# Grouped attention: the norm by half block, two scalings instead of four, turned outputs copied by ScalarE

## The chip, the cores and the metric

The kernel runs on one core of one Trainium2 chip. The metric is device time in microseconds (us) of one execution; a kernel's time is the median of several executions. The engines are TensorE (PE, with its weight loads PEld), VectorE (DVE), ScalarE (ACT), GpSimd (POOL) and SyncE (SP), which issues most DMAs.

## The reference

The program computes a decoder of two layers on x of 64 sequences x 64 steps x 256 channels, float32. Each layer adds three blocks to x, each on a layer norm of x:

```python
x = x + _L0_attn_ref(_layernorm(x), ...)    # Mamba-2 scan
x = x + _L0_xattn_ref(_layernorm(x), ctx_512, ...)   # latent cross attention
x = x + _L0_ffn_ref(_layernorm(x), ...)     # mixture of 7 experts, 2 chosen, 1 shared
x = x + _L1_attn_ref(_layernorm(x), ...)    # RWKV scan (WKV)
x = x + _L1_xattn_ref(_layernorm(x), ctx_512, ctx_512)
x = x + _L1_ffn_ref(_layernorm(x), ...)     # grouped mixture, 8 of 64 chosen
```

The change is in the fifth of these, the grouped attention of layer 1, which has no weights: 32 query heads of 8 channels share 8 key and value heads, taken from the 64 channels of ctx_512:

```python
qh = q.reshape(B, S, KV, G, D).transpose(0, 2, 3, 1, 4)     # KV 8, G 4, D 8
kh = k.reshape(B, S, KV, D).transpose(0, 2, 1, 3)
vh = v.reshape(B, S, KV, D).transpose(0, 2, 1, 3)
weights = jax.nn.softmax(jnp.einsum('bkgsd,bktd->bkgst', qh, kh) / scale, axis=-1)
out = jnp.einsum('bkgst,bktd->bkgsd', weights, vh)
```

## The kernel before

The residual x stays in SBUF for the whole program: 4096 tokens as 32 tiles of 128 tokens on the partitions. Four tiles are a block (8 blocks of 512 tokens), two tiles a half (16 halves of 256). A tile is two sequences of 64 steps.

The work of a layer is written as many Python generators, called streams. `Plan.play` (L204) runs them against each other while the program is built: each stream says at its `yield` which marks, which PSUM banks or which rank it waits for, the planner keeps an estimated time at which each engine is free, and the ready stream that could begin first continues, ties by rank. The order in which instructions are issued on each engine is fixed in that way; on the chip an engine takes its own instructions in that order. So an edit to one stream can move the instructions of all others. All instructions are recorded through one helper, so the profile gives line 62 for each; they are told apart by the names of their tiles.

Layer 1 (`layer1`, L1664) plays together: the WKV streams (`wkv_front`, `wkv_scan`, names wk_ and wn_), one pair for each half; the grouped attention (`gqa_front`, one for each block, and `gqa_tile`, one for each tile); the mixture (`ffn_front`, names fn_ and fr_; `ffn_half`, `ffn_gate`, `ffn_down`, names gu_ps, aT, acc); and the collection of layer 0's expert outputs by gathers of GpSimd (x_sb<-moe_ys). The mark ("scan", h) is set when WKV's result of half h is added to x, ("keys", b) when the keys kb of block b are there, ("gqa", n) when attention of tile n is added, ("ffn", n) when the mixture's result of tile n is added. `after` leaves out marks with a negative number. GQA_LEAD is 9: attention of tile n waits for the mixture of tile n-9.

`gqa_tile` (L1336) does for tile n:

- it waits for the block's keys, the half's scan, the attention of tile n-2 and the mixture of tile n-9;
- it calls `norm` (L287) for one tile: statistics gn_st and gn_mv on VectorE, variance plus epsilon gn_rs on VectorE, its power -1/2 on GpSimd, and gn_nm, minus the mean times that, on VectorE;
- GpSimd clears two columns of each query group in one of three buffers gqa_q, and scales x into it by four `tensor_scalar`, one for each of the four query heads g that share a key head (128 partitions x 64 columns each);
- `gqa_turned` (L1324): four PE transposes pq, copied to qT by ScalarE;
- 32 small score matmuls sc into four banks, whose maxima VectorE writes, negated, into the cleared columns of gqa_q; a second `gqa_turned` (qT2), so that the second score matmuls st contain the maximum; ScalarE's exponentials pT;
- eight matmuls pv with the values and a column of ones; VectorE copies the result from PSUM to oT; four transposes po; VectorE divides (rc, at); GpSimd adds to x.

`norm` takes the first tile and the number of tiles, keeps st in one buffer and mv, rs, nm in two, and yields between its steps. Other blocks call it for two or four tiles at a time.

Of the kernel before, what the change touches and what calls it, by code (L numbers as in the profile page):

```python
# [8 lines left out]
ALU = mybir.AluOpType  # L9
# [6 lines left out]
NT = TB // P  # L16
# [5 lines left out]
GQA_LEAD = 9  # L22
# [18 lines left out]
def bc(ap, axis, n):  # L41

    ap = ap.unsqueeze(axis)
    shape = list(ap.shape)
    shape[axis] = n
    return ap.to_broadcast(shape)
# [193 lines left out]
class Net:  # L240
# [1083 lines left out]
    def gqa_turned(self, wk, qa, tag):  # L1324
# [8 lines left out]
        yield [4]  # L1333
        return qT

    def gqa_tile(self, wk, w, n, f):  # L1336
        nc, te, v, gp = self.nc, self.nc.tensor, self.nc.vector, self.nc.gpsimd
        t = n % NT
        yield self.after(("keys", n // NT), ("scan", n // 2), ("gqa", n - 2), ("ffn", n - GQA_LEAD))
        r_ = {}  # L1340
        yield from self.norm(wk, n, 1, "gn", r_)
        qa = w["q"][n % len(w["q"])]
        gp.memset(qa.rearrange("p g k c -> p (g k) c")[:, :, 16:18], 0.0)
        xg = self.x[:, n].rearrange("p (k j g d) -> p g k j d", k=4, j=2, g=4)
        for g in range(4):
            gp.tensor_scalar(qa[:, g, :, 0:16].rearrange("p k (j d) -> p k j d", j=2), xg[:, g], r_["rs"], r_["nm"], ALU.mult, ALU.add)
        qT = yield from self.gqa_turned(wk, qa, "qT")

        sc = [self.mm([P, 4, 2, S], "sc") for _ in range(4)]
        for g in range(4):  # L1350
            for k in range(4):
                r = slice(32 * k, 32 * k + 32)
                for j in range(2):
                    te.matmul(sc[k][j * S:(j + 1) * S, g], qT[r, g, j * S:(j + 1) * S], f["kb"][r, 2 * t + j], start=True, stop=True)
        yield
        for k in range(4):
            v.tensor_reduce(qa[:, :, k, 16:18], sc[k], AX.X, ALU.max, negate=True)
        self.give(*sc)
        qT = yield from self.gqa_turned(wk, qa, "qT2")
        ps = [self.mm([P, 2, 4, S], "st") for _ in range(4)]  # L1360
        for j in range(2):
            for k in range(4):
                r = slice(32 * k, 32 * k + 32)
                te.matmul(ps[k][:, j], f["kb"][r, 2 * t + j].rearrange("p j t -> p (j t)"), qT[r, :, j * S:(j + 1) * S], start=True, stop=True)
        yield
        pT = wk.tile([P, 4, 2, 4 * S], F32, tag="pT", bufs=2, name="pT")
        for k in range(4):
            nc.scalar.activation(pT[:, k], ps[k].rearrange("p j g s -> p j (g s)"), AF.Exp, scale=8.0 ** -0.5)
        self.give(*ps)
        yield [1]  # L1370

        pv = self.mm([P, 4, 2, S], "pv")
        for j in range(2):
            for k in range(4):
                te.matmul(pv[k * 32:(k + 1) * 32, :, j], f["vb"][:, 2 * t + j, k].rearrange("p q d -> p (q d)"), pT[:, k, j],
                          start=True, stop=True)
        yield
        oT = wk.tile([P, 4, P], F32, tag="oT", bufs=2, name="oT")
        v.tensor_copy(oT, pv.rearrange("p g j s -> p g (j s)"))
        self.give(pv)  # L1380
        yield [1]
        po = self.mm([P, 4, 8, 16], "po")
        for g in range(4):
            te.transpose(po[:, g].rearrange("p k d -> p (k d)"), oT[:, g], self.ident)
        yield
        rc = wk.tile([P, 4, 8], F32, tag="rc", bufs=2, name="rc")
        v.reciprocal(rc, po[:, :, :, 8])
        at = wk.tile([P, D], F32, tag="at", bufs=2, name="at")
        v.tensor_mul(at.rearrange("p (k g d) -> p g k d", k=8, g=4), po[:, :, :, 0:8], bc(rc, 3, 8))
        self.give(po)  # L1390
        yield
        gp.tensor_add(self.x[:, n], self.x[:, n], at)
        self.plan.mark("gqa", n)
# [270 lines left out]
    def layer1(self, wk, w_wkv, w_gqa, w_ffn):  # L1664
        self.wkv_padded(wk, w_wkv)
        streams = [(0, self.shared(n)) for n in self.shared_left] + [(1, x) for x in [self.load_ffn(w_ffn), self.prep_ffn(wk, w_ffn)]]
        fs = [{} for _ in range(NH + NBLK)]
        streams += [(n, self.collect(n)) for n in range(NH)]
        for n in range(NH):
            streams += [(n, self.wkv_front(wk, w_wkv, n, fs[n])), (n, self.wkv_scan(wk, w_wkv, n, fs[n]))]  # L1670
        for b in range(NBLK):
            g = fs[NH + b]
            streams.append((2 * b, self.gqa_front(wk, w_gqa, b, g)))
            streams += [(2 * b + t // 2, self.gqa_tile(wk, w_gqa, NT * b + t, g)) for t in range(NT)]
        for i, (n0, nt) in enumerate(self.GROUPS):
            f = {}
            streams.append((n0 // 2, self.ffn_front(wk, w_ffn, i, n0, nt, f)))
            streams += [(h, self.ffn_half(wk, w_ffn, i, h, f)) for h in range(n0 // 2, (n0 + nt) // 2)]
        with self.tc.manual_schedule():
            self.plan.play(streams)  # L1680
# [113 lines left out]
```

## Time and profile before

| | us |
|---|---|
| median of 3 timed runs | 2126.09 (2123.85 to 2131.75) |
| the profiled execution | 2121.44 |
| its span, first to last instruction | 2119.7 |
| first instruction of grouped attention (gn_st) | starts at 1161.7 |
| last addition of grouped attention to x | starts at 2008.2 |

| engine | busy us in the span | share |
|---|---|---|
| TensorE, matmuls | 1933.7 | 91% |
| VectorE | 1343.7 | 63% |
| ScalarE | 791.1 | 37% |
| GpSimd | 845.6 | 40% |

In a timeline line the first number is the start in us, the second the time taken, then engine, line, operation, what is written and read, and the count; in brackets the idle time of the engine before it and what ended that. In a list of waits the instruction left of the arrow waited for the one on its right. In a table of stages each engine has its busy time and, in brackets, its instructions; then come the clock granted to TensorE (1.00 is full), the busy share of the DMA engines, and GB/s.

### The profile page before, as it was taken

How to read it: one execution, taken by the hardware profiler on the slowest of the kernel's cores; microseconds unless marked ns; L12 is line 12 of the kernel's file. 1: busy time of each engine (PE TensorE's matmuls, PEld its weight loads, DVE VectorE, ACT ScalarE, POOL GpSimd, SP SyncE). 2: the span in 40 equal slices, each digit the busy share in tenths (PEclk: the TensorE clock that was granted, in tenths of full speed). 3: DMA queues.
4: the chain of work that ended last, by engine and by line, in shares of the span. 5: the costliest groups of instructions: out<-in, count | busy, mean ns of one | idle time of the engine just before them, and what ended most of it. 6: DMA issues, size and time to landing. Idle time of an engine off the chain costs nothing. (4 is left out here: it accounts for less than half of the span.)

```text
span 2119.7 us, 36371 instructions
## 1 busy us (share of the span) xinstructions
PE 1933.7 (91%) x13735; PEld 1548.6 (73%) x13735; DVE 1343.7 (63%) x3149; ACT 791.1 (37%) x1439; POOL 845.6 (40%) x1045
## 2 busy tenths in 40 slices
PE   7989898898989897899988879989899999999998
PEld 6768677687778775688876557767677777777777
DVE  5667776767676773343336887877778676755331
ACT  3425343434334332244433423433334334243220
POOL 2332434343534423111126856667456334432211
PEclk9989999999899998999998879989999999999999
DMA  7963200000000001388844212121111101010010
GB/s 206 348 202 118 67 16 22 16 22 16 22 26 26 22 31 67 132 302 281 276 159 91 29 21 35 15 35 22 22 20 24 19 14 18 9 23 15 17 23 11
DMA packets 167807, 150.43 MB, mean 71 GB/s; under 512 B 76153, under 2 KB 155408, under 8 KB 167632
## 3 DMA queue, kind: packets, MB, share of 16 engines
q1 hardware_dynamic: 152464, 121.61, 19.6%
q0 software_dynamic: 15168, 26.50, 5.1%
q8 instruction: 109, 1.79, 0.3%
q14 instruction: 66, 0.54, 0.1%
HBM read 88.01 MB, written 60.04 MB: 70 GB/s over the span
## 5 line engine op out<-in xcount | busy, mean ns | idle before, releaser
L62 PE MATMUL gu_ps<-hT,ffn_gu 128*128 128x256 f32 x1408 | 337.0, 386 | 5.0 <-DVE gqa_q L62 4.1
L62 PEld LDWEIGHTS gu_ps<-hT,ffn_gu 128*128 128x128 f32 x1408 | 260.2, 192 | 50.4 <-issue 8.4
L62 PE MATMUL acc<-ffn_d,aT 128*128 128x256 f32 x704 | 166.0, 389 | 9.2 <-DVE aT L62 9.2
L62 POOL TENSOR_TENSOR aT<-aT,ffn_sc 128x512 f32<-128x512 f32 (+1 forms) x48 | 69.1, 1440 | 229.1 <-DVE aT L62 197.1
L62 PEld LDWEIGHTS acc<-ffn_d,aT 128*128 128x128 f32 x704 | 134.4, 194 | 34.3 <-DVE aT L62 10.7
L62 PE MATMUL proj<-sf_hT,w_in 128*128 128x256 f32 x640 | 148.2, 389 | 0.0
L62 ACT ACT_TABLE_LOAD x104 | 133.4, 1283 | 21.4 <-PE st L62 7.9
L62 PEld LDWEIGHTS proj<-sf_hT,w_in 128*128 128x128 f32 x640 | 121.7, 194 | 18.5 <-issue 1.8
L62 PE MATMUL po<-xa_vo,ctxT 128*128 128x256 f32 x512 | 121.8, 394 | 4.9 <-ACT ctxT L62 2.8
L62 ACT ACTIVATE aT<-gu_ps 128x512 f32<-128x512 f32 x96 | 48.7, 559 | 203.4 <-PE gu_ps L62 203.3
L62 DVE TENSOR_TENSOR aT<-aT,gu_ps 128x512 f32<-128x512 f32 x96 | 56.9, 633 | 106.2 <-ACT aT L62 106.2
L62 PE MATMUL q_ps<-xn_hT,xa_q 128*128 128x256 f32 x512 | 118.3, 386 | 2.5 <-DVE ctxT L62 1.3
L62 PEld LDWEIGHTS po<-xa_vo,ctxT 128*128 128x128 f32 x512 | 99.4, 198 | 23.1 <-ACT ctxT L62 7.8
L62 POOL DMA_INDIRECT x_sb<-moe_ys,left x64 | 106.6, 1665 | 23.3 <-issue 12.0
L62 PEld LDWEIGHTS q_ps<-xn_hT,xa_q 128*128 128x128 f32 x512 | 96.3, 192 | 22.0 <-ACT xn_hT L62 2.7
L62 POOL DMA_DIRECT2D moe_ys<-y x38 | 26.3, 692 | 207.0 <-ACT y L62 194.4
L62 DVE TENSOR_REDUCE gqa_q<-sc 128x8 f32<-128x512 f32 x128 | 79.3, 681 | 35.4 <-PE sc L62 35.4
L62 DVE TENSOR_TENSOR x_sb<-x_sb,po 128x256 f32<-128x256 f32 x64 | 26.5, 415 | 107.5 <-PE po L62 107.4
L62 DVE SCALAR_TENSOR_TENSOR sf_acc<-proj,ssm_vec,sf_acc 128x252 f32<-128x252 f32 (+2 forms) x192 | 87.3, 472 | 7.5 <-ACT sf_acc L62 3.0
L62 POOL TENSOR_TENSOR p<-p,sm 128x1024 f32<-128x1024 f32 x32 | 60.8, 1907 | 73.0 <-DVE sm L62 42.5
L62 POOL DMA_INDIRECT moe_hs<-moe_h,moe_slots x64 | 64.4, 1006 | 56.9 <-ACT gT L62 27.1
L62 ACT COPY qT<-pq 128x512 f32<-128x512 f32 x64 | 37.4, 586 | 115.2 <-PE pq L62 115.2
(367 smaller groups left out, 4338.7 us busy)
## 6 DMA issues: line engine op xcount, KB each, us to landing
moe_hs<-moe_zero SPq DMA_DIRECT2D x30, 1088.0 KB
pack<-in_moe_pack_dram SPq DMA_DIRECT2D x38, 770.0 KB
ht<-moe_hs SPq DMA_DIRECT2D x32, 272.0 KB
moe_ys<-y POOLq DMA_DIRECT2D x32, 256.0 KB, 5.7
bias<-moe_bias SPq DMA_DIRECT2D x38, 128.0 KB
x_sb<-in_x_dram SPq DMA_DIRECT2D x8, 512.0 KB
moe_hT<-mr_hT SPq DMA_DIRECT2D x8, 512.0 KB
sh_hT<-moe_hT SPq DMA_DIRECT2D x16, 256.0 KB
```

Of the source, the lines that this page charges most:

```text
L62: return do(*a, **k)
```

## The change

The norm of grouped attention gets a stream of its own for each half, `gqa_norm`, started in `layer1` with rank h. It waits for the half's scan and for attention of tile 2h-3, norms both tiles at once and sets the mark ("normed", h), for which the two tiles wait in place of the scan. The queries are scaled in two instructions, one for each value of j (the half of the key heads), of 16 runs of 8 columns. The turned outputs oT are copied by ScalarE.

```diff
+    def gqa_norm(self, wk, h, f):
+        yield self.after(("scan", h), ("gqa", 2 * h - 3))
+        r = f["norm", h] = {}
+        yield from self.norm(wk, 2 * h, 2, "gn", r)
+        self.plan.mark("normed", h)
+
     def gqa_tile(self, wk, w, n, f):
         nc, te, v, gp = self.nc, self.nc.tensor, self.nc.vector, self.nc.gpsimd
         t = n % NT
-        yield self.after(("keys", n // NT), ("scan", n // 2), ("gqa", n - 2), ("ffn", n - GQA_LEAD))
-        r_ = {}
-        yield from self.norm(wk, n, 1, "gn", r_)
+        yield self.after(("keys", n // NT), ("normed", n // 2), ("gqa", n - 2), ("ffn", n - GQA_LEAD))
+        rs, nm = (f["norm", n // 2][k][:, n % 2:n % 2 + 1] for k in ("rs", "nm"))
...
-        for g in range(4):
-            gp.tensor_scalar(qa[:, g, :, 0:16].rearrange("p k (j d) -> p k j d", j=2), xg[:, g], r_["rs"], r_["nm"], ALU.mult, ALU.add)
+        for j in range(2):
+            gp.tensor_scalar(qa[:, :, :, 8 * j:8 * j + 8], xg[:, :, :, j], rs, nm, ALU.mult, ALU.add)
...
         oT = wk.tile([P, 4, P], F32, tag="oT", bufs=2, name="oT")
-        v.tensor_copy(oT, pv.rearrange("p g j s -> p g (j s)"))
+        nc.scalar.copy(oT, pv.rearrange("p g j s -> p g (j s)"))
...
             streams.append((2 * b, self.gqa_front(wk, w_gqa, b, g)))
+            streams += [(h, self.gqa_norm(wk, h, g)) for h in (2 * b, 2 * b + 1)]
             streams += [(2 * b + t // 2, self.gqa_tile(wk, w_gqa, NT * b + t, g)) for t in range(NT)]
```

As the planner then writes it, ScalarE has 32 copies and 6 table loads more (110 instead of 104), VectorE 64 instructions fewer, GpSimd 80 fewer, TensorE as many as before. TensorE's order is the same up to the first transpose of grouped attention, differs from there, and is the same again from the last tile's attention to the end.

## The prediction

> **What bounds the kernel now.** I read the page's first two blocks, then busy time and granted clock by stage, then the list of what TensorE (PE) waited for, then PE's timeline around the waits that the change touches.
>
> ```profile
> span 2119.7 us, 36371 instructions
> ...
> PE 1933.7 (91%) x13735; PEld 1548.6 (73%) x13735; DVE 1343.7 (63%) x3149; ACT 791.1 (37%) x1439; POOL 845.6 (40%) x1045
> ...
> DVE  5667776767676773343336887877778676755331
> POOL 2332434343534423111126856667456334432211
> PEclk9989999999899998999998879989999999999999
> ```
>
> PE is busy 91% of the span. From the 22nd slice (53 us each) VectorE (DVE) and GpSimd (POOL) are at their fullest, and the clock row dips: there layer 1 begins, where grouped attention (names gn_, gqa_q, qT, sc, st, pT, oT) runs among the WKV scan (wk_) and the mixture (gu_ps, acc, fr_). The first gn_ instruction starts at 1161.7 us, the last attention result is added at 2008. The view of busy time by stage (us, then PE, PEld, DVE, ACT, POOL, granted clock, DMA) cuts that stretch:
>
> ```profile
> 1160.00:1300.00 140.00, 112.70 (x944) 83.93 (x943) 112.69 (x219) 52.68 (x97) 91.41 (x97) 0.85 0.19 27
> 1300.00:1400.00 100.00, 87.79 (x767) 67.70 (x766) 82.76 (x159) 39.81 (x69) 67.85 (x69) 0.93 0.17 25
> 1400.00:1560.00 160.00, 149.80 (x1264) 116.02 (x1265) 119.82 (x211) 61.22 (x103) 96.53 (x99) 0.98 0.17 26
> ...
> 1160.00:2008.00 848.00, 785.18 (x6608) 609.81 (x6607) 602.67 (x1165) 324.02 (x545) 430.53 (x478) 0.96 0.13 21
> 2008.00:2119.70 111.70, 103.00 (x564) 84.88 (x562) 29.85 (x71) 17.23 (x29) 16.94 (x15) 1.00 0.07 17
> ```
>
> The change touches no matmul. So it can win only what PE loses in the 848 us: 848 - 785.2 = 62.8 us of idle time, and clock. A stage's clock loss I take as busy time times what is missing to 1.00: 0.15 x 112.7 + 0.07 x 87.8 + 0.02 x 149.8 = 26.0 us in the three rows shown, and 4.9 us in the stages 1560 to 1660 (0.98) and 1660 to 1760 (0.97), 30.9 us in all. Ceiling: 94 us, 4.4%. The last 112 us are mixture matmuls alone, in the same order in the changed program; nothing is to be had there. What PE waited for from 1160 to 2008 (us in total, times, longest):
>
> ```profile
> PE pq L62 <- POOL gqa_q L62: 11.8, 6, 4.0
> PE wk_po L62 <- POOL wk_o L62: 8.3, 5, 3.0
> PE weT_ps L62 <- DVE fr_sc L62: 5.5, 1, 5.5
> ...
> PE pk L62 <- DVE wk_mix L62: 4.3, 1, 4.3
> ...
> PE po L62 <- DVE oT L62: 3.9, 4, 1.5
> PE st L62 <- ACT aT L62: 3.1, 3, 1.1
> ```
>
> The largest item is the one that the change is about: the transposes pq waiting for the scaled queries. All waits for ScalarE (ACT) together are 8.2 us.
>
> **Part by part.** Durations are medians of their own rows in the trace unless a mean is named.
>
> 1) The norm by half. Per tile it is statistics 0.42, aggregate 0.18, add 0.15 on DVE, power 0.56 on POOL, product 0.16 on DVE: 1.47 us, about 2 with the hops between engines. Statistics stay 32. Of add and product 32 + 32 become 16 + 16 (DVE -16 x 0.31 = -5.0 us), of power 32 become 16 with two columns (nearest row: sn_rs, 0.71 mean, against 0.66 mean for one column: POOL 21.1 - 11.3 = -9.8 us). What matters more is when it runs: it waits for the half's scan and for attention of tile 2h-3, no longer for the block's keys, for tile n-2 or for the mixture's tile n-9. The long waits in which PE met unfinished queries:
>
> ```profile
> 1259.99 1.44 PE L62 MATMUL pq<-ident,gqa_q 128*128 128x128 f32 x4 [3.16 <-POOL gqa_q L62]
> 1377.52 4.54 PE L62 MATMUL acc<-ffn_d,aT 128*128 128x256 f32 x12 [4.08 <-DVE aT L62]
> 1388.31 1.22 PE L62 MATMUL pq<-ident,gqa_q 128*128 128x128 f32 x3 [4.04 <-POOL gqa_q L62]
> 1524.54 0.33 PE L62 MATMUL pq<-ident,gqa_q 128*128 128x128 f32 x1 [2.08 <-POOL gqa_q L62]
> 1641.51 2.86 PE L62 MATMUL acc<-ffn_d,aT 128*128 128x256 f32 x12
> ```
>
> At 1260 the statistics start only at 1256.2, after the block's second key copy (1253.0), although the scan's result was added at 1245.6. At 1388 the scan was added at 1359.0 and the keys were there at 1372.2, yet the statistics stand behind the mixture's sum and start at 1382.7; then the two products stand behind six mixture instructions (1384.3 to 1386.8) while POOL idles 1.96 us. At 1524 the chain of one tile runs from 1519.9 on, beside the addition of an earlier tile on POOL (1519.0 to 1520.5), and on POOL both its power and its scaling stand behind a WKV instruction. In the changed order of DVE the first of these norms stands right behind the scan's sum, ahead of the keys, and the second ahead of the keys. So 3.16 + 4.04 and 0.32 (the last transpose) + 2.08 and 0.47 = 10.1 us are within reach. At the fourth place (1203.4, 1.70 us) the norm has no earlier start. Bounds 0 and 11.8; I take 7, since the next wait behind each place will keep some.
>
> 2) Two scalings instead of four. Now 4 x 0.39 = 1.57 us a tile (mean 0.47). No row shows this strided 128x128 form: from below it is one 128x64 instruction (0.39), from above two of them (0.78); between the 128x64 row and fr_h (128x256, 0.55) a straight line gives 0.45, which I take, since fr_h is the same operation on POOL. So 2 x 0.45 = 0.9, a gain of 0.67 a tile and 21 us of POOL in all. PE's first transpose now waits for both, 0.5 later than today; the last, which the copy qT needs, is ready 0.67 earlier. This is inside the 7 of part 1; at the upper end of 0.78 the part gains nothing and the 7 becomes 6.
>
> 3) The turned outputs on ACT. DVE loses 32 x 0.69 = 22 us, ACT gains 32 copies at 0.59 (row of qT, same 128x512 from PSUM) = 18.8 us. The planned program also has 110 table loads instead of 104: 6 x 1.28 = 7.7. The wait po <- oT (3.9 in four places) can go from all to nothing: at 1187, 1226, 1232 and 1403 the copy stood behind DVE work such as the 3.3 us reciprocal, behind ACT it stands after a few copies. I take -2. On ACT, busy 324 of 848 us, the cover is its waiting for PE; bounds 0 and 18.8 + 7.7 = 26.5, taken near the low end at +2, since PE waited for ACT only 8.2 us in all. If that cover fails see the second rival.
>
> 4) DVE's relief on the path. From 1160 to 1300 DVE is busy 80%, and the chain runs through it (weT_ps <- fr_sc, pk <- wk_mix above). It loses there four oT copies (2.7 us) and 3 x 0.31 = 0.9: bounds 0 and 3.6, taken 2. After 1560 PE is 96% busy or more; there the relief is worth nothing.
>
> 5) Added chain: where a half's norm cannot run early, its first tile waits for a second tile's statistics (0.42 + 0.18) and a longer power (0.05 to 0.15): 0.7 us. Bounds 0 and 16 x 0.7 = 11; taken for the first two halves, +1 rounded down from 1.4. In the queues of DVE and POOL nothing is put ahead of others but these instructions; no DMA moves with them.
>
> 6) Clock. 30.9 us lost beside 62.8 us idle is 0.49 us for each us of idle. In the rows above 12 acc matmuls take 4.54 us after a gap and 2.86 at full clock. Parts 1, 3 and 4 remove 11 us of idle, so bounds 0 and 0.49 x 19.3 = 9.5 (11.8 + 3.9 + 3.6 removed); taken 4.
>
> The Trainium skill, page "TensorE: Matmul & The Clock Gate", section "Part 1: The HAM clock gate", speaks against this term: it says that the clock falls only after an idle window of about 3.4 us. By it only gaps longer than that count, which among the ones reached here is the 4.04 alone, worth some 1.7 us as in the acc rows; the sum would be 2.3 us less. The trace does not quite agree: 1200 to 1220 shows a clock of 0.74 after gaps of 3.04, 1.70 and 1.01.
>
> **Sum:** -7 - 2 + 2 - 2 + 1 - 4 = -12 us. The profiled span of 2119.7 becomes 2107.7; the profiled run is 1.7 longer than its span (2121.4) and the median of the three timed runs 4.7 longer than that run (2126.1), so the median becomes **2114 us**, -0.56%.
>
> **Rivals.** First, **the idle time moves on** (no change). Filling one gap brings PE sooner to the next releaser: DVE's maxima (gqa_q, 11.5 us of PE's waits), wk_o (8.3), wk_mix (4.3), none of which the change shortens; and the order written by the planner is another one from the first attention tile on, with gaps of its own. For it: past 1560 PE idles only about 3% and the mixture fills in. Against it: two of the three places had their data 10 us and more before the norm began. It would leave only parts 3 and 4, about -3: 2123.
>
> Second, **ScalarE's queue** (slower). ACT works strictly in order; a turned-output copy waits for pv, and what stands behind it waits too. In the changed order 14 of the 32 copies are followed, at once or after a table load, by a Silu (aT) or by the exponentials pT that PE needs. If all 26.5 us of added ACT work land in front of PE, and parts 1, 4, 5, 6 (-12) hold, the result is +14.5: 2140.6. It decides from the point where PE's waits for ACT grow by 12 us, from 8.2 to 20; slower by 0.5% it is from 8.2 to 31. Against it: ACT idles 62% of the stretch, mostly for PE.
>
> That the change does not do what it says, a norm that is not early, falls with the first rival: parts 1 and 6 go and 5 stays.
>
> **How the numbers follow.** Forecast 0.60, first rival 0.23, second 0.17. The forecast's own range goes from all bounds on the gaining side, -11.8 - 3.9 - 3.6 - 9.5 = -28.8, to -4: 2097 to 2122. The range to hold 8 in 10 reaches to the second rival: 2097 to 2141. A measurement of this kernel can tell about 0.5% (10.6 us) from no change. Faster by more than that: 0.52 of the forecast's 0.60. Slower: 0.14 of the second rival and 0.02 of the first. The rest, 0.32, within.
>
> **What would show it.** In the profile after: gqa_q on POOL x64 near 0.45 us (step 2); PE's wait pq <- POOL gqa_q down from 11.8 to about 5 (1); oT under ACT at 0.59, po <- oT about 2 (3); PE's waits for ACT near 10 (3); idle PE in the attention stretch near 52 instead of 62.8 and the clock of its first 140 us above 0.85 (4, 6). It would be wrong if the idle time stays near 62 under other names, or if waits for ACT pass 20.

## The result, and the profile after

The changed kernel takes 2139.2 us (median of six runs, 2134.5 to 2141.9) against 2126.4 (2120.3 to 2131.8) for the kernel before on the same chip: a ratio of 1.0061, interval 1.0041 to 1.0081. It is 12.8 us slower; the forecast was 12 us faster. The profiled execution took 2138.35 us, that of before 2121.44.

The first two blocks of its page:

```profile
span 2136.5 us, 36296 instructions
...
PE 1941.4 (91%) x13735; PEld 1551.0 (73%) x13735; DVE 1341.2 (63%) x3085; ACT 816.2 (38%) x1477; POOL 816.3 (38%) x965
...
DVE  5667776777677764343336887798667767824331
POOL 2332434353543423111127766655454324412211
PEclk9989999999899998999999899989999999999999
```

POOL is relieved by 29 us and ACT has 25 more, six table loads (7.7 us) among it. PE, whose 13735 matmuls are the same, is busy 7.7 us longer. To see where, I cut both traces at the first instruction of grouped attention and at its last addition to x, since the part ahead of it, which the change can't reach, already differs by 4.3 us between these two executions (one and the same addition there starts at 1105.9 us in before and at 1108.3 in after). The table of stages, first of before, then of after (PE, PEld, DVE, ACT, POOL, clock, DMA, GB/s):

```profile
1161.65:2008.15 846.50, 783.68 (x6601) 608.49 (x6600) 602.05 (x1163) 324.02 (x545) 430.13 (x477) 0.96 0.13 21
```

```profile
1165.98:2023.44 857.46, 788.13 (x6601) 608.50 (x6600) 599.34 (x1099) 348.73 (x583) 400.01 (x398) 0.96 0.13 21
1160.00:1300.00 140.00, 116.36 (x975) 86.94 (x976) 112.59 (x216) 57.21 (x103) 91.39 (x84) 0.90 0.20 28
1300.00:1400.00 100.00, 85.83 (x655) 63.57 (x654) 80.37 (x125) 43.91 (x72) 70.37 (x63) 0.91 0.17 25
1400.00:1560.00 160.00, 148.51 (x1267) 114.06 (x1266) 125.22 (x225) 65.34 (x113) 78.29 (x76) 0.97 0.15 24
```

The same 6601 matmuls take 11.0 us longer: PE idles 69.3 us (857.46 - 788.13) instead of 62.8, which is 6.5, and is busy 4.4 us longer. Another 1.5 us lie behind the stretch. 11.0 + 1.5 = 12.5 us is close to the 12.8 between the medians. What PE waited for in after, from 1160 to 2025 (us in total, times, longest):

```profile
PE wk_po L62 <- POOL wk_o L62: 13.4, 5, 5.2
PE pk L62 <- DVE wk_mix L62: 8.1, 9, 3.3
PE weT_ps L62 <- DVE gqa_q L62: 7.8, 2, 4.2
PE wk_hT L62 <- ACT wk_h L62: 7.1, 5, 3.9
PE weT_ps L62 <- DVE fr_sc L62: 5.7, 2, 5.5
PE pq L62 <- POOL gqa_q L62: 4.0, 4, 2.1
...
PE gu_ps L62 <- ACT pT L62: 2.8, 3, 1.4
...
PE po L62 <- ACT oT L62: 0.7, 1, 0.7
```

The waits that the change aims at did fall: pq for the scaled queries from 11.8 to 4.0 us, po for oT from 3.9 to 0.7. But wk_po grew from 8.3 to 13.4, and weT_ps <- gqa_q (7.8) and wk_hT <- wk_h (7.1) are new. None of these waits is for an instruction that the change edited. (pk only seems to have grown from 4.3 to 8.1: 3.3 of it is one wait at 1159.91 us, ahead of the stretch; inside it pk's is 4.8.) How such a wait comes about is seen at weT_ps, the transposes of the mixture's gate. PE's timeline of after:

```profile
1602.33 0.38 PE L62 MATMUL pl<-ident,fr_lT 128*128 128x128 f32 x2
1602.55 1.89 PE L62 MATMUL gu_ps<-hT,ffn_gu 128*128 128x256 f32 x8
1604.37 1.21 PE L62 MATMUL sc<-kb,qT 32*64 32x128 f32 x64
1609.81 0.63 PE L62 MATMUL weT_ps<-ident,fr_sc 128*64 128x128 f32 x4 [4.24 <-DVE gqa_q L62]
```

and of before, at the same step of the mixture:

```profile
1602.41 0.38 PE L62 MATMUL pl<-ident,fr_lT 128*128 128x128 f32 x2
1602.62 1.04 PE L62 MATMUL pq<-ident,gqa_q 128*128 128x128 f32 x8
1603.50 1.89 PE L62 MATMUL gu_ps<-hT,ffn_gu 128*128 128x256 f32 x8
1605.23 1.89 PE L62 MATMUL wk_po<-wkv_o,wk_o 128*128 128x256 f32 x8
1606.95 0.68 PE L62 MATMUL wk_hT<-ident,wk_h 128*128 128x128 f32 x4
1607.47 1.89 PE L62 MATMUL gu_ps<-hT,ffn_gu 128*128 128x256 f32 x8
1609.30 1.15 PE L62 MATMUL gu_ps<-fr_smT,ffn_mgu 32*128 32x256 f32 x16
1610.37 0.62 PE L62 MATMUL weT_ps<-ident,fr_sc 128*64 128x128 f32 x4
```

Between pl and weT_ps the router works on ACT and DVE; in after that takes until 1609.15, 6.4 us after pl, and none of its instructions (fr_s, fr_sc, fr_m, fr_rest) is one of the changed ones. In before PE has 7.7 us of other matmuls put between the two; in after it has 3, and stands still for 4.24. The releaser named is gqa_q, the four maxima that stand behind the router's last fr_sc on DVE (1609.08, 2.47 us for the four): the first one ends near 1609.7 and frees a PSUM bank of the scores, which weT_ps seems to take. That is the last 0.6 us; the rest it would have waited for fr_sc anyway. The long gaps tell the same: before has 8 gaps of 2 us and more in the stretch, 28.3 us together, after has 11 and 40.1.

Two theories to test. **Order:** the changed instructions are worth little; what cost 12.8 us is the order that the planner dealt anew once it was told of them, with gaps of its own. (A deal is here the order that the planner writes from one set of estimates and streams.) **ScalarE** (the prediction's second rival): the copies and table loads on ACT hold PE. For ScalarE speaks that PE's waits for ACT rose from 8.2 to 15.5 us.

The planner makes them separable. It only needs to be told of an instruction (`nc.enter`) to place everything else; the instruction that is then issued may be another (`.real`). So a kernel can keep one order and issue the other kernel's instructions. Where a kernel below is said to have an order, each engine has the same list of instructions in the same order, but for the changed ones and what the compiler adds.

### The profile page after: what moved, and what is told of

It reads as the page before. It is cut to its first block, busy times and chain, and to the rows that moved or that the text cites. A ratio compares the mean times of both kernels' runs of the same rounds, so it can differ in the third digit from the quotient of the medians.

```text
span 2136.5 us, 36296 instructions
## 1 busy us (share of the span) xinstructions
PE 1941.4 (91%) x13735; PEld 1551.0 (73%) x13735; DVE 1341.2 (63%) x3085; ACT 816.2 (38%) x1477; POOL 816.3 (38%) x965
## 5 line engine op out<-in xcount | busy, mean ns | idle before, releaser
L62 ACT ACTIVATE pT<-st 128x512 f32<-128x512 f32 x128 | 66.1, 603 | 61.9 <-PE st L62 61.8
```

Source lines behind the costliest of these rows:

```text
L62: return do(*a, **k)
```

## Experiments

Ratios are to the kernel before, run on the same chip; its medians there were 2122.9, 2124.4, 2124.4, 2126.1 and 2126.6 us. "The stretch" is the time from the first instruction of grouped attention to its last addition to x in the profiled execution: 846.5 us before, 857.5 after.

### Instructions and order apart

The changed copy and scaling in the order of before:

```diff
-            gp.tensor_scalar(qa[:, g, :, 0:16]..., xg[:, g], r_["rs"], r_["nm"], ...)
+            nc.enter("gpsimd", "tensor_scalar", (qa[:, g, :, 0:16]..., xg[:, g], r_["rs"], r_["nm"], ...), {})
+        for j in range(2):
+            gp.real.tensor_scalar(qa[:, :, :, 8 * j:8 * j + 8], xg[:, :, :, j], r_["rs"], r_["nm"], ...)
...
-        v.tensor_copy(oT, ...)
+        nc.enter("vector", "tensor_copy", (oT, ...), {})
+        nc.scalar.real.copy(oT, ...)
```

> The order of every queue is that of the kernel before, instruction by instruction; only the changed instructions differ: oT is copied by ScalarE and the queries are scaled in two instructions instead of four. The norm stays one for each tile. Theory 'order' (the changed instructions themselves gain a little; the loss of 12.8 us comes from the order that the planner dealt anew when it was told of them): 2118 to 2127 us, the same as before or some us faster, because pq's wait for POOL's gqa_q shrinks by about 0.6 us a tile where it is met and nothing else moves. Theory 'ScalarE' (the copies and the table loads that they bring hold PE, wherever they are put): ScalarE has 32 x 0.59 = 19 us more work in the same places, so 2132 to 2140 us, and PE's waits for ACT in the attention stretch rise from 8.2 to over 14 us.

Measured: 2128.3 us, ratio 1.0027 (1.0014 to 1.0039), between the two theories. PE's waits for ACT rose to 17 us, which is what ScalarE asked for, but the time rose by some 5 us only. (The stretch is 843.2 us, 3.3 less than before, but the profiled execution was the fastest of the eight, 2122.6, so it says little.) wk_hT <- wk_h and weT_ps <- gqa_q, the new waits of after, are not among PE's waits here, and the table loads stay at 104.

The other way round, the order of the changed kernel (norm by half block included) with VectorE's copy and four scalings issued; the edit to after is the same one backwards.

> The order of every queue is that of the changed kernel, with the norm by half block where the change put it, but oT is copied by VectorE again and the queries are scaled in four instructions again. Theory 'order': the loss stays, 2135 to 2147 us (the four scalings put back cost up to 0.7 us a tile where pq waits for them). Theory 'ScalarE': ScalarE is rid of the copies, the loss goes, 2120 to 2130 us.

Measured: 2147.8 us, ratio 1.0117 (1.0100 to 1.0135), stretch 870.3, just above the range of theory "order". With the copies off ScalarE the loss does not go, it nearly doubles. What PE waited for, from 1160 to 2035:

```profile
PE wk_po L62 <- POOL wk_o L62: 11.4, 6, 4.0
PE po L62 <- DVE oT L1388: 7.9, 8, 3.1
PE wk_hT L62 <- ACT wk_h L62: 7.8, 6, 3.5
PE weT_ps L62 <- DVE gqa_q L62: 7.6, 2, 4.0
```

The waits that were new in after are here with the old copy and scaling, and were not in the old order with the new ones: they go with the order. So do PE's longer waits for ACT (15.5 us here as in after, with no oT copy on it) and the six table loads (110 here). ScalarE falls; the loss sits in the order. (The norm by half block is part of this run; it is in the deal at 95 below too, which is faster than before.) In this order the copy is better on ScalarE than on VectorE: here po waits 7.9 us for oT, against 0.7 in after.

### A new deal with no instruction changed

One number of the planner's cost table is changed at the start of `layer1`, nothing else:

```diff
     def layer1(self, wk, w_wkv, w_gqa, w_ffn):
+        self.plan.COST = dict(Plan.COST, vector=(101, 1.17))    # was (100, 1.17); the second nudge is (100, 1.18)
```

> The kernel before, with not one instruction of the attention changed: only the planner's estimate of a VectorE instruction's fixed cost is 101 ns instead of 100 ns in this part of the program, which makes it deal the order anew from part of the way through the attention. Theory 'order' (a new deal is a lottery of its own): the time moves by anything between -15 and +15 us, and by over 3 us more likely than not. Theory 'ScalarE' and any other that puts the loss on the changed instructions: within 3 us of before, 2123 to 2130 us.

> As the nudge before it, with the planner's estimate of VectorE's cost for each element at 1.18 instead of 1.17 and the fixed part untouched; the order is dealt anew from about where the real change begins to deal it anew. Theory 'order': anything between -15 and +15 us, by over 3 us more likely than not, and not the same as the first nudge. Theories that put the loss on the changed instructions: 2123 to 2130 us.

Measured: 2116.6 us, ratio 0.9972 (0.9961 to 0.9983), and 2124.7, 1.0014 (1.0001 to 1.0026). The first moved by 6 us with no instruction changed. The second missed the "more likely than not over 3 us": 3 us by its ratio, 1.4 in the stretch. Two draws alone do not show a spread that reaches 13 us.

### Each instruction by itself, in the order of before

The scaling alone and the copy alone: each one half of the first diff.

> Every queue in the order of the kernel before, VectorE copies oT as before, and only the scaling is in two instructions. Two theories on the 5 us that the two changed kinds of instruction cost in the old order. Theory 'first quarter': with four scalings the turning of the first of the four query groups starts after 0.39 us and the others follow as they are scaled; with two, which each cover all four groups, it starts after 0.9 us and all four turnings (0.6 to 1.1 us) come behind it, so nothing is won: +0 to +3 us against before. Theory of the prediction (0.7 us less for each tile that waits): -4 to -1 us.

> Every queue in the order of the kernel before, four scalings as before, and only the copy of oT is done by ScalarE, in the place that the old order gave to VectorE's copy. If the copy behind ScalarE's other work is what cost the 5 us: +3 to +6 us against before, po's waits for oT about 9 us against 3.9. If the scaling was it: -2 to +1 us.

Measured: the scaling 2129.1 us, ratio 1.0023 (1.0009 to 1.0037); the copy 2124.0, ratio 0.9999 (0.9987 to 1.0012). The copy costs nothing, though with it PE waits more for ACT (15.0 us in all), above all here:

```profile
PE po L62 <- ACT oT L1380: 8.9, 6, 2.7
PE wk_po L62 <- POOL wk_o L62: 6.6, 5, 2.0
```

po's wait is 5 us longer than before, and other waits such as wk_po's (8.3 before) are shorter; that VectorE's relief is the reason is not shown. This is what the prediction's second rival spoke of, waits for ACT up by 7, and it costs nothing. The scaling in two gained nothing and lost about 5 us, more than either theory had. With it PE's wait for the queries grew from 11.8 us to

```profile
PE pq L62 <- POOL gqa_q L1348: 13.8, 4, 4.5
```

At each of the four places where PE stood longest, the wait ahead of the first transpose is longer (2.70 us instead of 1.70, 3.62 instead of 3.16, 4.52 instead of 4.04, 2.98 instead of 2.08), and the shorter waits between transposes (0.32 and 0.47) are gone. So far the theory "first quarter" shows; but near 1260 us the turning of all four groups still ends sooner, at 1261.04 instead of 1261.43, the scaling having started 0.1 us earlier. PE's idle time in the stretch is 3.0 us longer (65.8 against 62.8). Where the rest of the 5 us comes from stays open.

The norm by half block alone in the order of before: the planner is told of the norm of each tile; where it puts a half's first, the instructions for both tiles are issued, where it puts the second, none.

```diff
-                nc.vector.bn_stats(st[:, t], self.x[:, n0 + t])
+                nc.enter("vector", "bn_stats", (st[:, t], self.x[:, n0 + t]), {})
...
+            if r["at"] == 0:
+                r["at"] = 1
+                for t in range(2):
+                    nc.vector.real.bn_stats(s2[:, t], self.x[:, 2 * h + t])
...
```

> Every queue in the order of the kernel before; four scalings, VectorE's copy. Only the norm is by half block: where the old order has a half's first norm, one norm of both tiles is issued (four statistics instructions, one of each of the others), and where it has the second, nothing. Theory 'order': the norm in itself is a small gain, 2118 to 2125 us, since the odd tile's three steps on VectorE and POOL are gone and nothing is moved; pq's wait for POOL's gqa_q falls from 11.8 to 6 to 9 us. If the norm by half costs in itself (the first tile waits for the statistics of both, about 0.7 us more, and its pq is the one that waits): 2126 to 2132 us.

Measured: 2120.2 us, ratio 0.9984 (0.9973 to 0.9996): a gain of 3.4 us, with 48 instructions fewer (16 additions and 16 products on VectorE, 16 powers on GpSimd). The wait of pq, expected at 6 to 9, did not fall, though: 12.2 us against 11.8. In the old place the first tile's norm is as late as before.

### The norm and the scaling in a free deal

The norm by half with nothing else changed, then norm and scaling with VectorE's copy, each dealt by the planner. The edits are those parts of the change.

> Only the norm by half block, dealt anew by the planner; four scalings and VectorE's copy. Theory 'order': anywhere from 2108 to 2138 us, with pq's wait for POOL's gqa_q down to 3 to 6 us whatever the total. Theory 'ScalarE': faster than before by the 7 to 12 us of the waits removed, 2111 to 2116 us.

> The changed kernel with the copy given back to VectorE and the planner left free to deal the order for it. Theory 'order': anywhere from 2108 to 2145 us, and not tied to the result of the norm alone. Theory 'ScalarE': 2110 to 2125 us, since the copies are off ScalarE.

Measured: 2136.6 us, ratio 1.0042 (1.0027 to 1.0057), and 2131.4, ratio 1.0034 (1.0021 to 1.0048). The norm alone loses 9 us in its own deal, where it gains 3.4 in the old order; pq's wait for POOL is down to 5.9 us all the same. No ScalarE copy is in either. With the scaling added, pq's wait is 10.1 us and the total is not larger: the total is not tied to the wait that was aimed at.

### Other deals of the changed kernel, and of the kernel before

The changed kernel with the nudge at 95 and at 105 instead of 100, then one more execution of the first (the name of that run speaks of four scalings; it has two), the kernel before with the same two nudges, and the changed kernel at 101, which moves only 8 rows of PE's 7580 and one copy on ScalarE.

> The changed kernel, with the planner's estimate of a VectorE instruction's fixed cost at 95 instead of 100 ns in this part of the program; the order is dealt anew from about a third of the way through the attention. Theory 'order': 12.8 us is one draw of a spread, so another deal of the same instructions lands elsewhere, anywhere from 2115 to 2145 us, and by over 4 us from 2139 more likely than not. Theory that the changed instructions cost the time in any order: 2135 to 2143 us.

> As the one before it, with the estimate at 105 ns; dealt anew from earlier on. Theory 'order': anywhere from 2115 to 2145 us, by over 4 us from 2139 more likely than not, and not tied to the result at 95 ns. Theory that the changed instructions cost the time in any order: 2135 to 2143 us.

> The changed kernel nudged by 95 ns once more, for a look at another execution of it: 2109 to 2121 us, the span of its eight runs.

> The kernel before, with the planner's estimate at 95 ns, as in the nudged changed kernel that ran at 2114 us. Theory 'order': another draw, 2110 to 2140 us, and not lower for this estimate than for another. Rival: the estimate of 95 ns is simply a better one for the planner, and with it the kernel before gains as much as the changed one did (25 us), under 2112 us.

> The kernel before, with the planner's estimate at 105 ns. Theory 'order': another draw, 2110 to 2145 us. If the estimate itself has a direction (95 ns made the kernel before slower by 18 us and the changed one faster by 25), nothing follows for 105 ns; a value beyond 2126 on the slow side again would say that the kernel before stands on a lucky draw.

> The changed kernel with the planner's estimate at 101 ns, which moves 8 rows of PE's list of 7580 and none on VectorE or POOL: a near null. Theory 'order': the time stays that of the changed kernel, 2136 to 2142 us, since the order stays. If runs of one program differ by their placement or by the chip rather than by the order: anywhere from 2115 to 2145 us.

All deals side by side:

| VectorE cost told to the planner | instructions of before | instructions of after |
|---|---|---|
| (100, 1.17), as it is | 1 | 1.0061 (1.0041 to 1.0081) |
| (101, 1.17) | 0.9972 (0.9961 to 0.9983) | 1.0055 (1.0036 to 1.0073), 8 rows moved |
| (100, 1.18) | 1.0014 (1.0001 to 1.0026) | not run |
| (95, 1.17) | 1.0089 (1.0072 to 1.0107) | 0.9952 (0.9933 to 0.9971) |
| (105, 1.17) | 1.0000 (0.9987 to 1.0014) | 1.0031 (1.0019 to 1.0044) |

The instructions of after land at 2139, 2114 or 2131 us; those of before at 2126, 2117, 2125, 2145 or 2128. The further execution at 95 took 2111.0. The kernel before at 95 lies above the range that was expected of it (2110 to 2140), after at 95 just below its own (2115 to 2145). Where only 8 rows move the time stays (2138.1), so it is the order and not the build. The estimate of 95 is no better one as such: it made the kernel before 18 us slower. The mean ratio is 1.0015 over the five deals of before (5.0075 / 5) and 1.0015 over the three of after that differ (3.0044 / 3). With so few draws, which share their first part, that shows no gain and no loss of the change itself.

What the better deal of the same instructions looks like, in the stretch table and in the list of waits of the kernel nudged to 95:

```profile
1158.01:1992.70 834.69, 776.44 (x6601) 603.43 (x6600) 586.29 (x1099) 344.02 (x579) 401.41 (x398) 0.97 0.13 21
```

```profile
PE wk_po L62 <- POOL wk_o L62: 11.2, 4, 5.3
PE pq L62 <- POOL gqa_q L62: 7.1, 7, 2.1
...
PE weT_ps L62 <- DVE gqa_q L62: 2.0, 1, 2.0
```

The profiled execution is the fastest of its eight (2109.1 us; their median is 2114.1). The stretch is 22.8 us shorter than in after: PE idles 58.2 us instead of 69.3, and the same matmuls are busy 11.7 us less. The wait that the change was about, pq for POOL, is larger (7.1 against 4.0); weT_ps has 2.0 instead of 7.8, wk_hT <- ACT wk_h is gone from the upper part of the list. Its gate step has gu_ps matmuls ahead of weT_ps again:

```profile
1590.33 1.98 PE L62 MATMUL gu_ps<-hT,ffn_gu 128*128 128x256 f32 x8
1592.25 1.15 PE L62 MATMUL gu_ps<-fr_smT,ffn_mgu 32*128 32x256 f32 x16
1593.32 0.63 PE L62 MATMUL weT_ps<-ident,fr_sc 128*64 128x128 f32 x4
```

### What the scaling costs in other orders, and what is best

Four scalings put back, first in the order of after, then in the order at 95; last the norm by half in the order of the first nudge of before.

```diff
-            gp.tensor_scalar(qa[:, :, :, 8 * j:8 * j + 8], xg[:, :, :, j], rs, nm, ...)
+            nc.enter("gpsimd", "tensor_scalar", (qa[:, :, :, 8 * j:8 * j + 8], xg[:, :, :, j], rs, nm, ...), {})
+        for g in range(4):
+            gp.real.tensor_scalar(qa[:, g, :, 0:16]..., xg[:, g], rs, nm, ...)
```

> Every queue in the order of the changed kernel (norm by half block, ScalarE's copy), with only the four scalings put back for the two. In the order of before, two scalings instead of four were 4.9 us slower. If that price holds in any order: 4 to 6 us less than the changed kernel, 2133 to 2136 us. If it holds only in the order of before, because there the first of the four turnings is what PE has next: 2136 to 2142 us, as the changed kernel. If four are the slower ones here, as the 25 us of the kernel with four scalings and VectorE's copy in this order would have it: 2142 to 2148 us, and the rest is the copy's.

> The changed kernel nudged by 95 ns, every queue in that order, with the four scalings put back. Two scalings cost 4.9 us in the order of before and nothing measurable in that of the changed kernel. In this order PE waits 7.1 us in seven places for POOL's gqa_q, more than the 4.0 of the changed kernel and less than the 11.8 of before; so 0 to 4 us less than the 2114 us with two, 2108 to 2116 us.

> The same norm by half block, put into the order that the first nudge (101 ns) dealt, which ran 6 us faster than the kernel before. If the gain of the norm and that of the order add up: 6 us less than the kernel with the norm alone, 2110 to 2118 us, faster than both kernels of the case. If an order's gain is lost as soon as a few instructions in it change: 2118 to 2126 us.

Measured: 2138.8 us, ratio 1.0059 (1.0041 to 1.0076), the same as after; 2113.5, ratio 0.9943 (0.9917 to 0.9969), against 0.9952 with two; and 2117.3, ratio 0.9971 (0.9959 to 0.9984), against 0.9972 for that order without the norm. So two scalings are worth nothing in the two new orders (and lost 5 us in the old one), though pq's wait for POOL is longer with two than with four in both: 4.0 us against 3.0 in the order of after, 7.1 against 4.4 at 95. The norm's 3.4 us of the old order is not found in the nudged one, so the two gains are not seen to add up, though 2117.3 us lies at the end of the range that was expected if they do (2110 to 2118). The copy on ScalarE is worth nothing in the old order and about 12 us in that of after (1.0117 against 1.0059). That one and the same instruction has a different price in another order is clear of the intervals for the copy; for the scaling and the norm the intervals overlap. The kernels at 95, with two or four scalings, beat both kernels of the case; they can't be told from each other.

## Why the prediction was wrong

**Steps 1 to 3, the waits aimed at: the numbers came, the reasons only in part.** gqa_q on POOL x64 has a median of 0.453 us (forecast 0.45), pq's wait is 4.0 (about 5), oT on ACT takes 0.587 (0.59), po's wait is 0.7 (about 2). But that pq's wait falls does not take the change: in the four other deals of the kernel before it is 3.1, 5.8, 4.8 and 0.3 us; the 11.8 belonged to one order. That step 1's early norm shortened it is not shown; no run has it in a fixed order. Step 2 had the duration right and the sign of the wait wrong: in all three orders where both were run, pq waits longer with two scalings than with four. Step 3 holds in the order of after (0.7 us instead of 7.9 with VectorE's copy) and not in the old one, where po's wait grew from 3.9 to 8.9.

**The sum: wrong, and this is the step that failed.** It took -7, -2, +2, -2, +1 and -4 as if PE's list stayed and only the named waits shrank. It does not stay: from the first transpose of grouped attention on, the planner dealt another one, and that deal brought waits at wk_po, weT_ps and wk_hT for which no step had a term. Idle time in the stretch was to be near 52 us and is 69.3: the prediction's own sign of being wrong, idle time that stays under other names. In the old order held fixed the parts measure -3.4 us (norm), +4.9 (scaling) and about 0 (copy), so even there the sum was too hopeful; the norm's -7 stands against -3.4 without the early start, which exists only in a new order.

**The first rival named the cause and mis-sized it.** "The order written by the planner is another one [...] with gaps of its own" is what the runs show. But it was priced as if the new gaps would at most cancel the gain: 2123 (by about -3 for parts 3 and 4, which as listed add up to -2). What they can cost was not bounded at all. The deals measured here reach from -10 us (0.9952) to +19 (1.0089). That the range of 2097 to 2141 held 2139.2 is luck: it reached that far for the second rival, which is not what happened.

**The second rival, ScalarE's queue: refuted as the cause.** PE's waits for ACT came to 15.5 us, more than the 10 that were forecast and below the rival's mark of 20; the same 15.5 are there with no copy on ScalarE, and the 7.7 us of table loads in its price are not the copies' either (104 loads with the copies in the old order, 110 without them in the new). With no copy on ScalarE the same order is slower still (2147.8), with the copies in the old order nothing is lost (2124.0), and in the order at 95 the same 32 copies run in a kernel of 2114 us.

**Step 4**, VectorE's relief of 2 us, could not be told apart from the rest; the copy alone in the old order bounds it together with step 3 at -3 to +3 us (0.9987 to 1.0012).

**Step 5**, the added chain, shows in the old order at two of the four places: PE's wait is 0.2 and 0.3 us longer there with the norm by half.

**Step 6, the clock: not as summed.** The clock of the first 140 us rose to 0.90 from 0.85, as forecast. Yet over the stretch the mean clock is 0.96 in both, and busy time rose by 4.4 us. The number of long gaps does not decide it: after has three of over 3.4 us in those 140 us (5.17, 5.46 and 3.64), before has two (5.54 and 4.29), and after lost less. In before the clock stood at 0.50 from 1224.41 to 1244.89 us, in which PE was busy for 12.6 of 20.5 us, and from 1282.44 to 1285.85, with only gaps of 1.40 and 0.60 us, and three under 0.2 between them, close ahead of it. The Trainium skill, page "TensorE: Matmul & The Clock Gate", section "Part 1: The HAM clock gate", names an idle window of about 3.4 us as what brings the clock down. The gap of 1.40 does not agree with that, and the measurement decides. No run here isolates one gap.

## What to carry to other kernels

Where a planner or scheduler writes the order, an edit to one stream deals all streams anew, and the spread of such deals (here 1.2% between the fastest and the slowest with the instructions of before, 1.1% with those of after) is a cost of the edit that has to be in the range, larger than the terms that are worked out from the waits. Measure it first: nudge one number that the planner uses and see how far the unchanged kernel moves. To judge an edit itself, hold the order fixed by telling the planner of the old instruction and issuing the new one, and when the order turns out to be worth more than the edit, search over deals.

## What the runs showed of the hardware that was not expected

- The same 6601 matmuls of the stretch are busy 776.4 us in one order (at 95) and 795.8 in another (the order of after with VectorE's copy), with mean clocks of 0.97 and 0.96. A second execution at 95 has 774.1. An order costs not only idle time; between after and its deal at 95 half of the 22.8 us is in the matmuls' own time. The ends of matmuls are modelled, so what part of it is the clock and what part the pipeline is open.
- On GpSimd the strided scaling of 128x128 takes 0.453 us and that of 128x64 takes 0.392 (medians): twice the columns for 16% more. A power of two columns takes 0.724 in after, against 0.558 for one in before.
